# Summing graph messages: one 128-column lane window for each group of edges, in place of one or two block windows

## The chip, the core and the metric

The kernel runs on one core of a Trainium2 chip. The metric is the device time of a whole execution in microseconds; the median of the timed executions counts. A timed execution is not recorded. The profile comes from one further execution, recorded by the hardware profiler, whose own time is given beside its span below.

The engines are named as in the profile: PE (TensorE's matmuls) and PEld (its weight loads), DVE (VectorE), ACT (ScalarE), POOL (GpSimd), SP (SyncE, which here issues most of the DMAs).

## What is computed

A graph has 6250 nodes with 64 features and E = 206250 directed edges, sorted by destination. Four layers run one after another, each on the normalized output of the one before and each with a residual sum. The third is the one that matters here. It has a message for every edge, made of the edge's own 64 attributes and a transformed row of its source node, and takes for each node the root of the mean of the squared messages:

```python
Vp = jax.nn.leaky_relu(V @ pAw + pAb, NEG_SLOPE) @ pBw + pBb
x = jax.nn.relu(E @ mlp_w1 + mlp_b1)
x = jax.nn.relu(x @ mlp_w2 + mlp_b2)
scale = jax.nn.sigmoid(x @ Bw + Bb)
shift = x @ Cw + Cb
msg = scale * Vp[src] + shift
M = jnp.power(jnp.clip(msg, EPS, None), ALPHA)          # ALPHA = 2
ssum = jax.ops.segment_sum(M, dst, num_segments=n)
mean = ssum / jnp.maximum(cnt, 1.0)[:, None]
return jnp.power(mean, 1.0 / ALPHA)
```

The other three layers multiply node features by the graph's adjacency matrix (with degree norms); the last one does so three times.

## The kernel before

**Nodes, blocks and strips.** The 6250 nodes are padded to NP = 49 x 128: NB = 49 blocks of 128 nodes, in NC = 7 chunks of CB = 7 blocks. A node is a block and a lane (0 to 127) in it. The adjacency counts are first built as a dense bf16 matrix in DRAM, in 14 strips of 448 columns (A, made by L926 to L947). Layers one and two, and the last two rounds of layer four, go through the whole matrix with `gather`, whose matmuls are those of L733. A float32 feature block is held as three bf16 parts, so each product takes three matmuls.

**The edge loop.** Layer three runs over G = 202 groups of 128 x 8 = 1024 edges. It is a hand-made software pipeline: `slot(i)` issues, in a fixed order for PE, ACT and DVE (`manual_schedule`), one step of each of several groups. In slot i, SP loads the attributes of group i+2; POOL gathers the source rows of group i in eight indirect DMAs of 128 rows (`fetched`, L1226, into v, which has four buffers); PE transposes group i's attributes (L1234), does the first layer for group i-1 and the second for group i-2 (L1238), then gates and shifts for group i-3 (`gates_and_shifts`, L1248 and L1252, into p_bc, which has one buffer of two banks). DVE and ACT make the message of group i-4: L1261 multiplies gate and v and frees v, L1262 adds the shift and frees p_bc, L1263 clips, L1268 and L1269 square, L1320, L1321 and L1331 split the square into three bf16 parts (m3).

**The sum over nodes.** Edges are sorted by destination, so a group's nodes lie close together. `window(g)` gives the first block that a group can touch and how many (one or two), from the mean number of edges for each node and a margin DRIFT of 32 nodes. Before the loop, `rel_b` is made: the destination of each edge less the first node of its window, so 0 to 255 (L1077 to L1095, with a check that no edge lies outside). `compared_nodes` (L1274) compares it with a ramp of 256 (or 128) columns and gives a 0/1 matrix of 8 x 256 (or 8 x 128). In `summed`, a slot later, PE multiplies these columns by m3, in eight matmuls for each block (L1286), and accumulates in PSUM: each block has a p_s bank of its own (two in rotation), which stays open over all groups that touch the block. After the last of these, L1290 adds the three parts into H. With a chunk's last block, `finished` norms the chunk and makes it ready for layer four.

**Work beside it.** The loop carries other work, listed in `todo` and spread over the slots by `some_of`: checking that the matrix is symmetric (`crossed`: seven or fourteen transposes of L1137 into p_sum, then L1143 on DVE compares them with a piece of A), and the first round of layer four for the chunks that are done (`partial`: 21 matmuls of L733 into p_sum, then L1157 or L1159 adds to Y). p_sum has one bank. The piece and there tiles for it are loaded by SP. Of these there are 196 checks and 84 partial sums. How many are put into a slot depends on `ends`, the slot in which the next chunk is finished.

The slot's order on the three engines, as far as the change touches it, is: L1261 to L1263, transposes, readers of p_sum, first layer, squares, some of `todo`, L1274, L1320, L1321, second layer, gates and shifts, evictions, L1331, readers of p_sum, the rest of `todo`, `summed`.

[...]

Of the kernel before, what the change touches and what calls it, by code (L numbers as in the profile page):

```python
# [8 lines left out]
F32 = mybir.dt.float32  # L9
BF16 = mybir.dt.bfloat16  # L10
# [3 lines left out]
OP = mybir.AluOpType  # L14
AX = mybir.AxisListType

P = 128
N = 6250
D = 64
NB = 49  # L20
NP = NB * P
CB = 7
# [3 lines left out]
J = 8  # L26
G = -(-E // (P * J))
# [564 lines left out]
CW = 448  # L592
CS = NP // CW
SG = 8
DRIFT = 32


def window(g):

    per = N / E  # L600
    lo = max(int(g * P * J * per) - DRIFT, 0) // P
    hi = min(int((g + 1) * P * J * per) + DRIFT, NP - 1) // P
    return lo, hi - lo + 1


@with_exitstack
def fast(ctx, tc, bad, x, src, dst, edge_attr, W3, b3, W4, b4, w1, b1, w2, b2, Bw, Bb, Cw, Cb,
# [432 lines left out]
    with ExitStack() as ph:  # L1040
# [37 lines left out]
        width = tpool.tile([P, G], F32, name="width")  # L1078
        for t, value in ((origin, lambda g: window(g)[0] * P), (width, lambda g: window(g)[1] * P)):
            g0 = 0  # L1080
            for g in range(1, G + 1):
                if g == G or value(g) != value(g0):
                    nc.gpsimd.memset(t[:, g0:g], float(value(g0)))  # L1083
                    g0 = g
        rel = tpool.tile([P, G, J], F32, name="rel")
        nc.vector.tensor_tensor(rel, dst_g, origin.unsqueeze(2).to_broadcast([P, G, J]),
                                op=OP.subtract)
        rel_b = cpool.tile([P, G, J], BF16, name="rel_b")
        nc.vector.tensor_copy(rel_b, rel)
        off = tpool.tile([P, G, J], F32, name="off")  # L1090
        nc.vector.tensor_tensor(off, rel, width.unsqueeze(2).to_broadcast([P, G, J]), op=OP.is_ge)
        nc.vector.tensor_scalar(rel, rel, 0.0, None, op0=OP.is_lt)
        nc.vector.tensor_add(off, off, rel)
        nc.vector.tensor_reduce(missed[:, 1:2], off.rearrange("p g j -> p (g j)"), axis=AX.X,
                                op=OP.add)  # L1095
        count = cpool.tile([P, 2 * P, J], BF16, name="count")
        nc.gpsimd.iota(count, pattern=[[1, 2 * P], [0, J]], base=0, channel_multiplier=0,
                       allow_small_or_imprecise_dtypes=True)

        before.close()  # L1100
        mpool = ph.enter_context(tc.tile_pool(name="mpool", bufs=3))
        ps_a = ph.enter_context(tc.tile_pool(name="ps_a", bufs=1, space=PSUM))
        ps_s = ph.enter_context(tc.tile_pool(name="ps_s", bufs=2, space=PSUM))
        n1 = stat.tile([P, NB], F32, name="n1")
        nc.vector.tensor_scalar_max(n1, deg_dst, 1.0)
        nc.vector.reciprocal(n1, n1)
# [17 lines left out]
        def crossed(n, i, k, b):  # L1124
            if b % ROWS == 0:
                held["there"] = mpool.tile([P, ROWS, 2, CW], BF16, name="there", bufs=2)
                m = min(ROWS, CB - b)
                for h in range(2):
                    nc.sync.dma_start(held["there"][:, :m, h, :],
                                      A[2 * i + h][:, k * CB + b:k * CB + b + m, :])  # L1130

            p = ps_a.tile([P, 512], F32, name="p_sum").bitcast(BF16).rearrange(
                "p (a q) -> p a q", q=P)[:, :CB, :]
            for q in (slice(0, P),) if b != CB // 2 else (slice(0, D), slice(D, P)):
                half, lo = divmod(b * P + q.start, CW)
                for a in range(CB):
                    nc.tensor.transpose(p[q, a, :], held[half][:, a, lo:lo + q.stop - q.start],  # L1137
                                        ident_b)
            there = held["there"][:, b % ROWS].rearrange("p h w -> p (h w)")

            def compared():
                junk = mpool.tile([P, CB * P], BF16, name="junk", bufs=1)
                nc.vector.scalar_tensor_tensor(  # L1143
                    junk, p.rearrange("p a q -> p (a q)"), 0.0, there, op0=OP.add,
                    op1=OP.not_equal, accum_out=unlike[:, n:n + 1])

            return compared

        def partial(i, s):

            p = ps_a.tile([P, 512], F32, name="p_sum")
            for b in range(CB):
                spread(p, U3, i * CB + b, held[s % 2][:, b, :], CW, i * CB, CB)

            def added():
                if i == 0:
                    nc.vector.tensor_copy(Y[:, s, :], p[:, :CW])  # L1157
# [47 lines left out]

        plan(FIRST, False)
        last = {b: g for g in range(G) for b in range(window(g)[0], sum(window(g)))}
        ends = [last[c * CB + CB - 1] for c in range(NC)]
        acc = {}

        BC_AT, M_AT, SUM_AT = 3, 4, 5
        of = [{} for _ in range(G)]
        ends = [e + SUM_AT for e in ends]

        def loaded(g):
            of[g]["e"] = mpool.tile([P, J * D], F32, name="e")
# [49 lines left out]
            nc.scalar.activation(m, m, AF.Square)  # L1269

        def compared_nodes(g):
            nb = window(g)[1]
            to = of[g]["to"] = mpool.tile([P, 2 * P, J], BF16, name="to")
            nc.vector.tensor_tensor(  # L1274
                to[:, :nb * P, :], count[:, :nb * P, :],
                rel_b[:, g, :].unsqueeze(1).to_broadcast([P, nb * P, J]), op=OP.is_equal)

        def summed(g):
            b0, nb = window(g)
            m3, to = of[g].pop("m3"), of[g].pop("to")  # L1280
            for b in range(b0, b0 + nb):
                begins = b not in acc
                if begins:
                    acc[b] = ps_s.tile([P, 512], F32, name="p_s")
                for j in range(J):
                    nc.tensor.matmul(acc[b][:, :3 * D], to[:, (b - b0) * P:(b - b0 + 1) * P, j],  # L1286
                                     m3[:, j].rearrange("p t f -> p (t f)"),
                                     start=(begins and j == 0), stop=(last[b] == g and j == J - 1))
# [48 lines left out]
        loaded(0)  # L1337
        loaded(1)
        with tc.manual_schedule(engines={ET.PE, ET.Activation, ET.DVE}):
            for i in range(G + SUM_AT):  # L1340
                slot(i)
            read_them()

# [101 lines left out]
```

## Time and profile before

| | |
|---|---|
| timed executions | 3750.78, 3750.81, 3745.49 us; median 3750.78 |
| recorded execution | 4268.4 us, span 4266.6 us |
| mean granted TensorE clock, recorded | 0.863 of full speed; 0.80 from 1132 to 3749 us |
| first gather of the edge loop starts | 1132.5 us |
| last gather of the edge loop ends | 3748.9 us |
| last sum over nodes, L1290 | 3779.3 us |
| busy from 1132 to 3749 us (2617 us) | PE 1889.5, DVE 1146.7, ACT 863.9, POOL 1632.4 us |

The recorded execution is 518 us longer than the timed ones, so a sum made from its durations has to be carried over. The profile's group rows read: line, engine, operation, output and inputs with sizes, count, then busy time and mean nanoseconds of one, then the idle time of the engine just before them and what ended most of it. "issue" is a wait that nothing in the profile explains. A row of waits gives the total, the number and the longest; a row of the timeline gives start, length, engine, line, operation, count, and in brackets the idle time before it.

The edge loop is the middle of the page's forty slices, some 12th to 35th: PE's digit is 6 or 7 there, DVE's and POOL's are 4 and 6, and the granted clock moves between 0.6 and 0.8. In the stretches before and after, PE is at 9 with L733.

### The profile page before, as it was taken

To read this page: it belongs to the slowest core of one execution; us is meant where nothing else is said; L and a number is where in the kernel's file an instruction comes from. 1 tells how busy PE (TensorE), PEld (TensorE's weight loads), DVE (VectorE), ACT (ScalarE), POOL (GpSimd) and SP (SyncE) were. 2 spreads that over 40 slices of the span, in tenths; PEclk is the share of its full clock that TensorE was granted. 3 is DMA by queue.
4 is the path that set the end of the run, shared out by engine and by line. 5 is a ranking of instruction groups with operands and counts; after the bars stand their busy time and mean duration, and the time that the engine had idled before them with its cause. 6 is when DMAs were issued, how large, how long until landed. Compare 5 with 4: busy or idle time off the path is not lost.

```text
span 4266.6 us, 59486 instructions
## 1 busy us (share of the span) xinstructions
PE 3314.6 (78%) x24499; PEld 1988.6 (47%) x24499; DVE 1874.4 (44%) x3013; ACT 1305.6 (31%) x2108; POOL 1693.1 (40%) x1822
## 2 busy tenths in 40 slices
PE   0599989999476767677677777677777777789999
PEld 0366656555233434444443444344444444456665
DVE  5999942311243444435444444444444444450100
ACT  0577740111033333333333333333333333320000
POOL 4000000000366666655665666566566656610000
PEclk9799999999677778888887888788878878799999
DMA  3244449778732223333233333233323323269997
GB/s 103 90 187 173 198 202 421 288 319 339 106 82 73 73 69 92 83 100 85 72 98 85 88 85 103 67 86 89 99 71 102 96 76 88 73 231 369 376 363 299
DMA packets 278029, 650.45 MB, mean 152 GB/s; under 512 B 106505, under 2 KB 158787, under 8 KB 275699
## 3 DMA queue, kind: packets, MB, share of 16 engines
q1 hardware_dynamic: 220036, 584.91, 37.9%
q0 software_dynamic: 54112, 58.92, 7.3%
q8 instruction: 194, 3.18, 0.3%
q10 hardware_dynamic: 3600, 2.73, 0.3%
q14 instruction: 87, 0.71, 0.1%
HBM read 562.82 MB, written 83.58 MB: 152 GB/s over the span
## 4 chain that ended last, share of the span: by engine, by line
PE 56%; DVE 13%; issue 13%; another core or an unknown queue 8%; ACT 4%; DMA 3%; POOL 2%; DVEq 0%; ACTq 0%; SPq 0%; POOLq 0%
PE p_sum L733 28%; PE p_bc L1252 7%; PE p L1238 6%; PE p_s L1286 5%; PE p_a L935 3%; PE p_bc L1248 2%; DVE junk L1143 2%; DVE m L1261 2%; PE p_node L724 2%; PE p_e L1234 2%; DVE m L1262 2%; PE p_sum L1137 1%; POOL v L1226 1%; ACT h L1242 1%
## 5 line engine op out<-in xcount | busy, mean ns | idle before, releaser
L1226 POOL DMA_INDIRECT v<-Vp_dram,src_g x1616 | 1632.4, 1010 | 1019.9 <-DVE m L1261 510.6
L733 PE MATMUL p_sum<-piece,U 128*64 128x448 bf16 x10290 | 1111.0, 368 | 194.9 <-issue 133.4
L733 PEld LDWEIGHTS <-U 128*64 128x64 bf16 x12348 | 721.5, 113 | 728.0 <-issue 254.3
L1252 PE MATMUL p_bc<-BC,h 128*128 128x256 f32 x1616 | 534.6, 451 | 57.7 <-issue 56.2
L1286 PE MATMUL p_s<-m,to 128*128 128x192 bf16 x2816 | 352.9, 279 | 119.4 <-issue 118.7
L1252 PEld LDWEIGHTS p_bc<-BC,h 128*128 128x128 f32 x1616 | 308.9, 212 | 206.9 <-issue 179.9
L1083 POOL MEMSET origin<- 128x4 f32 (+3 forms) x49 | 1.7, 100 | 970.6 <-PE p_sum L733 970.6
L1286 PEld LDWEIGHTS <-to 128*128 128x128 bf16 x2816 | 301.1, 150 | 178.3 <-issue 172.1
L1261 DVE TENSOR_TENSOR m<-gate,v 128x512 f32<-128x512 f32 x202 | 139.9, 692 | 503.9 <-ACT gate L1257 288.1
L1242 ACT ACTIVATE h<-p,b_c 128x512 f32<-128x512 f32 x404 | 262.4, 685 | 245.9 <-remote 172.5
L939 ACT ACTIVATE strip<-p_a 128x784 bf16<-128x784 f32 x392 | 301.6, 820 | 89.8 <-PE p_a L935 88.5
L1143 DVE SCALAR_TENSOR_TENSOR junk<-p_sum,there 128x896 bf16<-128x896 bf16 x196 | 212.5, 1084 | 263.2 <-remote 196.1
L1238 PE MATMUL p<-h,w_d 128*128 128x512 f32 x404 | 254.7, 714 | 75.0 <-ACT h L1242 50.5
L1137 PE MATMUL p_sum<-ident_b,piece 128*128 128x128 bf16 (+1 forms) x1568 | 134.8, 235 | 209.8 <-DVE junk L1143 133.9
L1268 ACT ACTIVATE m<-m 128x512 bf16<-128x512 f32 x202 | 127.3, 630 | 505.8 <-DVE m L1263 398.4
L1137 PEld LDWEIGHTS <-piece 128*128 128x128 bf16 (+1 forms) x1568 | 108.5, 109 | 322.3 <-issue 265.9
L1238 PE MATMUL p<-eT,w_d 128*128 128x512 f32 x404 | 241.2, 679 | 16.4 <-issue 12.4
L1321 ACT ACTIVATE m<-m 128x512 bf16<-128x512 f32 x202 | 127.2, 630 | 370.3 <-DVE m L1320 285.7
L974 ACT ACTIVATE y<-p_sum 128x448 f32<-128x448 f32 x56 | 30.5, 544 | 678.7 <-PE p_sum L733 678.7
L926 DVE TENSOR_TENSOR lo<-count,key 128x2048 bf16<-128x2048 bf16 x196 | 238.1, 1215 | 0.0
L733 PE MATMUL p_sum<-strip,U 128*64 128x448 bf16 x2058 | 236.0, 358 | 0.4 <-ACT strip L939 0.4
L1274 DVE TENSOR_TENSOR to<-count,rel_b 128x2048 bf16<-128x2048 bf16 (+1 forms) x202 | 218.2, 1080 | 0.0
(172 smaller groups left out, 2993.8 us busy)
## 6 DMA issues: line engine op xcount, KB each, us to landing
piece<-A SPq DMA_DIRECT2D x498, 784.0 KB
A<-strip SPq DMA_DIRECT2D x14, 5488.0 KB
e<-in_edge_attr SPq DMA_DIRECT2D x202, 256.0 KB
v<-Vp_dram,src_g POOLq DMA_INDIRECT x1616
there<-A SPq DMA_DIRECT2D x56, 448.0 KB
there<-A SPq DMA_DIRECT2D x56, 336.0 KB
pairs<-pair SPq DMA_DIRECT2D x1, 1616.0 KB
Vp_dram<-v SPq DMA_DIRECT2D x7, 224.0 KB
```

The costliest lines, as they stand in the source:

```text
L733: nc.tensor.matmul(p[half * D:(half + 1) * D, :w], U3[:, b, k, :], at_block, start=(i < 2), stop=(i >= 3 * n - 2))
L926: nc.vector.tensor_tensor(t, of.unsqueeze(1).to_broadcast(t.shape), key[:, k, at:at + GB].rearrange("p (h j) -> p h j", j=GQ) .unsqueeze(2 ...
L939: nc.scalar.activation(strip[:, :, col:col + 2 * SG].rearrange("p b (j l) -> p b j l", l=2), p[:, :, :2 * NB].rearrange("p j (b l) -> p b ...
L1137: nc.tensor.transpose(p[q, a, :], held[half][:, a, lo:lo + q.stop - q.start], ident_b)
L1143: nc.vector.scalar_tensor_tensor(junk, p.rearrange("p a q -> p (a q)"), 0.0, there, op0=OP.add, op1=OP.not_equal, accum_out=unlike[:, n:n ...
L1226: nc.gpsimd.indirect_dma_start(out=v[:, j, :], out_offset=None, in_=Vp_dram[:, :], in_offset=bass.IndirectOffsetOnAxis(ap=src_g[:, g, j:j ...
L1238: nc.tensor.matmul(of[g][p], w, of[g].pop(x), start=True, stop=True)
L1242: nc.scalar.activation(of[g][t], of[g].pop(p), **how)
L1252: nc.tensor.matmul(p_bc[:, 2 * q:2 * q + 2].rearrange("p j o f -> p (j o f)"), h2[:, q * P:(q + 1) * P], BC, start=False, stop=(k == 1))
L1261: nc.vector.tensor_mul(m, of[g].pop("gate"), of[g].pop("v"))
L1274: nc.vector.tensor_tensor(to[:, :nb * P, :], count[:, :nb * P, :], rel_b[:, g, :].unsqueeze(1).to_broadcast([P, nb * P, J]), op=OP.is_equal)
L1286: nc.tensor.matmul(acc[b][:, :3 * D], to[:, (b - b0) * P:(b - b0 + 1) * P, j], m3[:, j].rearrange("p t f -> p (t f)"), start=(begins and j ...
```

## The change

A group's window is now always 128 nodes wide and begins at a multiple of QN = 32 nodes. It covers one block, or the end of one and the beginning of the next (`halves`). The 0/1 matrix is made by the lane of the node in its own block (`lane`, 0 to 127, the same for either block), with 128 columns for every group. Eight matmuls sum the group into one PSUM bank, starting and stopping with the group. In the next slot (ADD_AT = 6, one after SUM_AT = 5), DVE adds the three parts into a tile r and adds r, times a mask, to one block of H or to two. The masks (`own`) hold one or zero for each lane: from the window's first lane on, a lane belongs to the first block, below it to the second. The first addition to a block writes it.

p_s becomes one bank, taken from the pool of the others, and p_sum gets two. `finished` is called in the slot after the last sum, behind `summed`. The loop has one slot more, and `ends` moves by one.

```diff
 def window(g):
     per = N / E
-    lo = max(int(g * P * J * per) - DRIFT, 0) // P
-    hi = min(int((g + 1) * P * J * per) + DRIFT, NP - 1) // P
-    return lo, hi - lo + 1
+    lo = max(int(g * P * J * per) - DRIFT, 0) // QN
+    hi = min(int((g + 1) * P * J * per) + DRIFT, NP - 1) // QN
+    assert hi - lo < P // QN
+    return lo
+
+def halves(g):
+    b, q = divmod(window(g), P // QN)
+    return [(b, q, P // QN)] + [(b + 1, 0, q)] * (q > 0 and b + 1 < NB)
...
-        rel_b = cpool.tile([P, G, J], BF16, name="rel_b")
-        nc.vector.tensor_copy(rel_b, rel)
         off = tpool.tile([P, G, J], F32, name="off")
-        nc.vector.tensor_tensor(off, rel, width.unsqueeze(2).to_broadcast([P, G, J]), op=OP.is_ge)
+        nc.vector.tensor_scalar(off, rel, float(P), None, op0=OP.is_ge)
...
+        nc.vector.tensor_scalar(dst_g, dst_g, P - 1, None, op0=OP.bitwise_and)
+        lane = cpool.tile([P, G, J], BF16, name="lane")
+        nc.vector.tensor_copy(lane, dst_g)
+        own = cpool.tile([P, P // QN, 2], F32, name="own")
+        nc.vector.memset(own[:, :, 0], 0.0)
+        for q in range(P // QN):
+            nc.vector.memset(own[q * QN:(q + 1) * QN, :q + 1, 0], 1.0)
+        nc.vector.tensor_scalar(own[:, :, 1], own[:, :, 0], -1.0, 1.0, op0=OP.mult, op1=OP.add)
...
-        ps_s = ph.enter_context(tc.tile_pool(name="ps_s", bufs=2, space=PSUM))
...
-            p = ps_a.tile([P, 512], F32, name="p_sum")
+            p = ps_a.tile([P, 512], F32, name="p_sum", bufs=2)
...
         def compared_nodes(g):
-            nb = window(g)[1]
-            to = of[g]["to"] = mpool.tile([P, 2 * P, J], BF16, name="to")
+            to = of[g]["to"] = mpool.tile([P, P, J], BF16, name="to")
             nc.vector.tensor_tensor(
-                to[:, :nb * P, :], count[:, :nb * P, :],
-                rel_b[:, g, :].unsqueeze(1).to_broadcast([P, nb * P, J]), op=OP.is_equal)
+                to, count, lane[:, g, :].unsqueeze(1).to_broadcast([P, P, J]), op=OP.is_equal)

         def summed(g):
-            b0, nb = window(g)
+            p = of[g]["p_s"] = ps_a.tile([P, 512], F32, name="p_s")[:, :3 * D]
             m3, to = of[g].pop("m3"), of[g].pop("to")
-            for b in range(b0, b0 + nb):
-                begins = b not in acc
-                if begins:
-                    acc[b] = ps_s.tile([P, 512], F32, name="p_s")
-                for j in range(J):
-                    nc.tensor.matmul(acc[b][:, :3 * D], to[:, (b - b0) * P:(b - b0 + 1) * P, j],
-                                     m3[:, j].rearrange("p t f -> p (t f)"),
-                                     start=(begins and j == 0), stop=(last[b] == g and j == J - 1))
-                if last[b] == g:
-                    nc.vector.tensor_reduce(
-                        H[:, b, :], acc[b][:, :3 * D].rearrange("p (t f) -> p f t", f=D),
-                        axis=AX.X, op=OP.add)
-                    if b % CB == CB - 1:
-                        finished(b // CB)
+            for j in range(J):
+                nc.tensor.matmul(p, to[:, :, j], m3[:, j].rearrange("p t f -> p (t f)"),
+                                 start=(j == 0), stop=(j == J - 1))
+
+        begun = set()
+
+        def added_to_nodes(g):
+            r = mpool.tile([P, D], F32, name="r_s")
+            nc.vector.tensor_reduce(r, of[g].pop("p_s").rearrange("p (t f) -> p f t", f=D),
+                                    axis=AX.X, op=OP.add)
+            for k, (b, q0, q1) in enumerate(halves(g)):
+                part = own[:, q1 if k else q0, k:k + 1]
+                if b in begun:
+                    nc.vector.scalar_tensor_tensor(H[:, b, :], r, part, H[:, b, :],
+                                                   op0=OP.mult, op1=OP.add)
+                else:
+                    nc.vector.tensor_scalar(H[:, b, :], r, part, None, op0=OP.mult)
+                    begun.add(b)
+            return [b // CB for b, _, _ in halves(g) if last[b] == g and b % CB == CB - 1]
...
                 nc.vector.tensor_sub(m, m, m3[:, :, 0, :])
                 nc.scalar.activation(m3[:, :, 1, :], m, AF.Copy)
+            done = added_to_nodes(i - ADD_AT) if at(ADD_AT) else []
             if at(2):
                 layer(i - 2, w2_d, "h1", "p_2")
...
             if at(SUM_AT):
                 summed(i - SUM_AT)
+            for c in done:
+                finished(c)
```

More of the change, by code (lines that the diff above doesn't have):

```diff
@@ L594 @@
 SG = 8
+QN = 32
 DRIFT = 32
@@ L1077, in fast @@
         origin = tpool.tile([P, G], F32, name="origin")
[L1078 to L1084, printed above, removed]
+        g0 = 0
+        for g in range(1, G + 1):
+            if g == G or window(g) != window(g0):
+                nc.gpsimd.memset(origin[:, g0:g], float(window(g0) * QN))
+                g0 = g
         rel = tpool.tile([P, G, J], F32, name="rel")
@@ L1095, in fast @@
                                 op=OP.add)
-        count = cpool.tile([P, 2 * P, J], BF16, name="count")
-        nc.gpsimd.iota(count, pattern=[[1, 2 * P], [0, J]], base=0, channel_multiplier=0,
+        nc.vector.tensor_scalar(dst_g, dst_g, P - 1, None, op0=OP.bitwise_and)
[6 more added lines that the diff above has]
+        nc.vector.tensor_scalar(own[:, :, 1], own[:, :, 0], -1.0, 1.0, op0=OP.mult, op1=OP.add)
+        count = cpool.tile([P, P, J], BF16, name="count")
+        nc.gpsimd.iota(count, pattern=[[1, P], [0, J]], base=0, channel_multiplier=0,
                        allow_small_or_imprecise_dtypes=True)
@@ L1130, in crossed @@
                                       A[2 * i + h][:, k * CB + b:k * CB + b + m, :])
-            p = ps_a.tile([P, 512], F32, name="p_sum").bitcast(BF16).rearrange(
+            p = ps_a.tile([P, 512], F32, name="p_sum", bufs=2).bitcast(BF16).rearrange(
                 "p (a q) -> p a q", q=P)[:, :CB, :]
@@ L1206, in fast @@
         plan(FIRST, False)
-        last = {b: g for g in range(G) for b in range(window(g)[0], sum(window(g)))}
+        last = {b: g for g in range(G) for b, _, _ in halves(g)}
         ends = [last[c * CB + CB - 1] for c in range(NC)]
-        acc = {}
-        BC_AT, M_AT, SUM_AT = 3, 4, 5
+        BC_AT, M_AT, SUM_AT, ADD_AT = 3, 4, 5, 6
         of = [{} for _ in range(G)]
-        ends = [e + SUM_AT for e in ends]
+        ends = [e + ADD_AT for e in ends]
         def loaded(g):
@@ L1339, in fast @@
         with tc.manual_schedule(engines={ET.PE, ET.Activation, ET.DVE}):
-            for i in range(G + SUM_AT):
+            for i in range(G + ADD_AT):
                 slot(i)
```

## The prediction

> **What bounds the kernel now.** I read the page first (engines, slices), then the groups of line 5, POOL's waits, the timeline of single slots of the edge loop, and the windows of the loop. The loop is where the change lies: it runs from the first row gather at 1132.5 us to 3790 us, 207 slots, one group of 1024 edges each.
>
> ```profile
> span 4266.6 us, 59486 instructions
> PE 3314.6 (78%) x24499; PEld 1988.6 (47%) x24499; DVE 1874.4 (44%) x3013; ACT 1305.6 (31%) x2108; POOL 1693.1 (40%) x1822
> ...
> L1226 POOL DMA_INDIRECT v<-Vp_dram,src_g x1616 | 1632.4, 1010 | 1019.9 <-DVE m L1261 510.6
> ...
> L1286 PE MATMUL p_s<-m,to 128*128 128x192 bf16 x2816 | 352.9, 279 | 119.4 <-issue 118.7
> ...
> L1137 PE MATMUL p_sum<-ident_b,piece 128*128 128x128 bf16 (+1 forms) x1568 | 134.8, 235 | 209.8 <-DVE junk L1143 133.9
> ...
> L1274 DVE TENSOR_TENSOR to<-count,rel_b 128x2048 bf16<-128x2048 bf16 (+1 forms) x202 | 218.2, 1080 | 0.0
> ```
>
> To see here: the matmuls that the change halves (L1286) are 2816 of 24499, PE also waits on one p_sum buffer (133.9 us behind the comparison L1143), and POOL's 1616 gathers have 1020 us of gaps, half of them waits for a v buffer. The next two views are POOL's waits and POOL's timeline near the end of the loop, where nothing holds it.
>
> ```profile
> POOL v L1226 <- DVE m L1261: 510.6, 95, 18.8
> POOL v L1226 <- issue: 453.0, 1457, 2.4
> ```
>
> ```profile
> 3732.55 0.95 POOL L1226 DMA_INDIRECT v<-Vp_dram,src_g  x1 [0.30 <-issue]
> 3733.81 0.94 POOL L1226 DMA_INDIRECT v<-Vp_dram,src_g  x1 [0.30 <-issue]
> 3735.05 0.95 POOL L1226 DMA_INDIRECT v<-Vp_dram,src_g  x1 [0.30 <-issue]
> 3736.31 1.46 POOL L1226 DMA_INDIRECT v<-Vp_dram,src_g  x1 [0.30 <-issue]
> 3738.07 0.95 POOL L1226 DMA_INDIRECT v<-Vp_dram,src_g  x1 [0.30 <-DVE m L1262]
> 3739.32 1.63 POOL L1226 DMA_INDIRECT v<-Vp_dram,src_g  x1 [0.30 <-issue]
> ```
>
> A gather goes out every 1.25 us, so POOL alone needs 8 x 1.25 = 10.0 us a slot, 2020 us in all, and 123 us more for gathers that last over 0.945 us (like the 1.46 and 1.63 above). In the recorded execution a slot takes 2617 / 202 = 13.0 us, because PE is late: in its timeline there are stretches where matmuls start at steps of some 0.70 us with nothing to wait for, each 10 to 20 us long:
>
> ```profile
> 2185.84 0.24 PE L1286 MATMUL p_s<-m,to 128*128 128x192 bf16 x1 [0.79 <-issue]
> 2186.54 0.39 PE L1286 MATMUL p_s<-m,to 128*128 128x192 bf16 x2 [0.46 <-issue]
> ...
> 2195.87 1.54 PE L1286 MATMUL p_s<-m,to 128*128 128x192 bf16 x16
> ```
>
> The same 16 matmuls take 1.54 us when PE runs freely (a whole slot then lasts 8 us: transposes at 2189.26, the next at 2197.25).
>
> **Recorded and timed execution differ, and this decides the forecast.** The recorded one took 4268.4 us, the timed ones 3750.8: 518 us less. Which execution is bound by what? Take POOL's waits for v buffers out of the recorded span: 4266.6 - 511 = 3756 us. Or build it up: 1132.5 before the first gather, 2020 of gathers at full pace, 517.7 from the last gather's end (3748.9) to the end: 3670, and 80 us of lengthened gathers reach the timed 3750. So I read the timed execution as one in which POOL hardly ever waits (10.4 us a slot) and PE, with some 8 us of work at full clock, has 2 us to spare. This is an inference from two sums, not a record of a timed run.
>
> [...] I laid each gather's start against VectorE's instructions in the timeline. Of 155 gathers that started while L1274 ran, 154 were lengthened, 76.6 us in all, each by about what was left of L1274; L1320, L1261 and L1331 (also two SBUF inputs) add 24 us. Of 163 that started in L1143, whose one input is in PSUM, 2 were. [...] the granted clock changes in multiples of 3.4 us between 0.5 and 1.0, with a mean of 0.80 in the loop.
>
> **The change, part by part**, for 202 groups. From the two forms of window(): 150 groups now have two blocks and 52 one (352 x 8 = 2816 matmuls); after, each has one set of 8, 1616, and 352 halves are added (49 of them first writes).
>
> PE: 1200 matmuls of L1286 with their loads go. 16 take 1.54 us at full clock (0.096 each) and 2.76 at half clock (0.172): 115 to 206 us; by the row, 1200 x 352.9/2816 = 150. A second p_sum bank (taken from p_s[...]) removes most of the 134 + 47 us for which L1137 and L733 wait for L1143. In the recorded execution, where PE is late, I expect 150 plus about half of 181, and the pace is then PE's own: 4266 - 240 = some 4030. In the timed one PE's share is hidden by POOL.
>
> DVE: the comparison L1274 falls from 218.2 to 202 x 0.684 (its 1024-element form) = 138, -80. The reduction of p_s runs 202 times in place of 49: 153 x 0.358 = +55. 303 scalar_tensor_tensor and 49 tensor_scalar on 64 elements are new; the trace has none so small, L688 takes 0.625 for 448 elements [...] from below 0.17 (the 7-element L680), from above 0.36 (as L1290): +79. In sum +54, 0.27 us a slot. They stand between L1320 and L1331, where DVE waits 0.70 us for ACT's L1321 in nearly every slot, so this covers most of it; uncovered it would be 0.8 us on a DVE that is 44% busy.
>
> New waits: the reduction waits for PE's sums of the slot before; behind it on DVE stand L1331 and the readers of p_sum. Those sums take 0.9 us and were issued before the transposes of the new slot, while DVE has three passes, L1143, L1274 and L1320 to do: no wait as a rule, at worst 0.5. PE's next sums wait for the reduction because p_s has one bank; ahead of them stand p_bc's 2.8 us on PE, about as long as DVE needs from L1262 to the reduction (0.43 + 1.3 of ACT + 0.69 + 0.36). I take 0, at worst 0.8 us a slot, with the next slot's transposes queued behind; POOL's 2 us cover that. At the end there is one slot more: +1 us, against 4 tail slots that lose 0.7 each: -2.
>
> Before the loop: rel_b's cast (0.98) goes, the width compare becomes a tensor_scalar (1.83 to 0.99), a bitwise and (1 to 1.8), a cast (0.98) and six tiny instructions come (0.6 to 1): +0 to +1.5 on the wait of the first gather. 194 memsets replace 49 + 97, done during the 8.6 us load of dst_g.
>
> POOL, the bound: where POOL is always running, a DVE instruction of length d, shorter than the pitch, lengthens gathers by d*d/(2 x 1.25) on average. L1274 before: 150 x 0.593 + 52 x 0.187 = 98.7, of which the trace shows 76.6; after: 202 x 0.187 = 37.8, scaled alike 29. Gain 47. The bound from below is 0 (the phase is fixed by when the rows land, and may be one where both lengths cost alike), from above 0.54 x 150 = 81. The new scalar_tensor_tensor have two SBUF inputs: 303 x 0.020 = 6, at most 68. Together -41, with +1 before the loop and -2 at the end: about -43. Timed: 3750.8 - 43 = 3708.
>
> **Rivals.**
> A (forecast), POOL's pace is the bound, 3708, own range 3675 to 3738. For it: both sums above. Against: 1.25 us a gather may be shorter when nothing records. Chance 0.52.
> B, PE sets the pace in timed runs too. Then PE's 150 and part of 181 count: -120 to -220, 3580 as its value. For it: 728 us in which PE is not busy in the loop's 2617, and the clock, in the recorded run. Against: 8 us of work a slot against 10. Chance 0.18.
> C, nothing to see: the lengthening only moves from L1274 to L1320, which now starts in its place, within 0.2%: 3750. Chance 0.11.
> D, slower: [...] PE gets 0.6 us less work a slot and new short waits ahead of its sums, idles longer in each 10.4 us slot[...]. The 8.0 us slot above becomes 8.3 on the mean (84 x 2.27 / 202 = 0.9 more for L733, 0.2 less for L1286, 0.4 less for its 14 transposes), and 7.7 after the change: PE fits under POOL down to a granted clock of 0.74; at 0.70 a slot takes 11.0, 0.6 x 202 = 120 us, less A's 43: 3828. For it: half clock in a fifth to a half of each stretch already. [...] Chance 0.19.
>
> **How the numbers follow.** I can tell 0.2% (7.5 us) from no change. Faster: 0.48 of A, B's 0.18, 0.02 of C: 0.68. Same: 0.04 of A and 0.08 of C: 0.12. Slower: 0.01 of C and D: 0.20. The range for 8 in 10 takes A and C whole, B down to 3585 and D up to 3795.
>
> **What would show it.** Right: L1286 with 1616 matmuls; L1274 all at 0.68; POOL's gathers over 0.96 us fewer, their mean down from 1010 to about 985 ns; L1137's wait on L1143 nearly gone; a recorded span near 4030, with POOL's waits on L1261 down by more than half. Wrong: a mean gather unchanged (C); a timed gain over 100 us (B); a lower granted clock in the loop, L1286 waiting for the new reduction, and POOL still waiting for L1261 (D).

## The result, and the profile after

| | before | after |
|---|---|---|
| median of 4 executions | 3750.14 us (3745.49 to 3750.81) | 3725.39 us (3719.05 to 3728.70) |
| ratio after / before | | 0.9932, 95% interval 0.9918 to 0.9947 |
| forecast | | 3708 us, a ratio of 0.989 |

The change gains 24.75 us, 0.7%. The forecast was a gain of 43 us. The recorded execution of the changed kernel (3727.58 us) is one of its four. The recorded execution shown of before (4268.4 us) was of a kind that one chip later showed in every execution of the three kernels that ran on it, so the profile after is set beside a second record of the kernel before, e0_before_again, whose execution took 3742.60 us (span 3740.8).

The page of the changed kernel: span, engines with busy time and instructions, then rows of groups (busy, mean ns of one, idle time before and what ended most of it).

```profile
span 3725.9 us, 57673 instructions
...
PE 3092.7 (83%) x23299; PEld 1853.5 (50%) x23299; DVE 1890.3 (51%) x3525; ACT 1282.9 (34%) x2108; POOL 1666.7 (45%) x1870
...
L1238 POOL DMA_INDIRECT v<-Vp_dram,src_g x1616 | 1606.2, 994 | 529.1 <-issue 460.8
...
L1260 PE MATMUL p_bc<-BC_b,ones 3*128 3x512 bf16 x404 | 182.0, 450 | 359.4 <-DVE m L1274 358.8
...
L1292 PE MATMUL p_s<-m,to 128*128 128x192 bf16 x1616 | 202.7, 278 | 1.1 <-DVE r_s L1300 0.4
```

The same rows of the page of e0_before_again:

```profile
span 3740.8 us, 59486 instructions
...
PE 3142.0 (84%) x24499; PEld 1914.6 (51%) x24499; DVE 1856.7 (50%) x3013; ACT 1290.4 (34%) x2108; POOL 1684.1 (45%) x1822
...
L1226 POOL DMA_INDIRECT v<-Vp_dram,src_g x1616 | 1623.4, 1005 | 528.0 <-issue 450.7
...
L1286 PE MATMUL p_s<-m,to 128*128 128x192 bf16 x2816 | 286.3, 256 | 0.0
...
L1248 PE MATMUL p_bc<-BC_b,ones 3*128 3x512 bf16 x404 | 177.3, 439 | 117.3 <-DVE m L1262 117.2
L1137 PE MATMUL p_sum<-ident_b,piece 128*128 128x128 bf16 (+1 forms) x1568 | 128.8, 235 | 174.3 <-DVE junk L1143 174.2
...
L1274 DVE TENSOR_TENSOR to<-count,rel_b 128x2048 bf16<-128x2048 bf16 (+1 forms) x202 | 219.2, 1085 | 0.0
```

PE lost 1200 matmuls and its 174 us wait for the single p_sum bank behind the comparison of L1143 (after, none is left at the transposes and 0.3 us at L742), and has in their place 242 us more of waiting for p_bc (117.2 to 358.8): what PE was relieved of, it waits for DVE at another place. The row that the span follows is POOL's. Its gathers fell from 1005 to 994 ns on the mean, in sum by 1623.4 - 1606.2 = 17.2 us. POOL's waits after the change (total, number of times, longest) show that nothing holds it:

```profile
POOL v L1238 <- issue: 460.8, 1512, 0.3
...
POOL v L1238 <- DMA piece<-A: 37.0, 1, 37.0
POOL v L1238 <- DMA v<-Vp_dram,src_g: 25.6, 84, 0.3
```

The 37.0 us stand once, ahead of the first gather. No other wait is longer than the 0.3 us before every gather, so none was for a buffer of v. So the span can be cut at the first start and the last end of the gathers, and the loop between them into the time by which gathers last over 0.945 us ("lengthening") and the rest. This works for every record taken where the kernel before takes 3750 us; the experiments are explained below.

| record, us | first gather | lengthening | rest of the loop | after the last gather | span |
|---|---|---|---|---|---|
| e0_before_again | 1126.2 | 98.4 | 2017.2 | 499.1 | 3740.8 |
| after | 1128.0 | 81.0 | 2017.4 | 499.5 | 3725.9 |
| e1_wide_compare | 1127.8 | 99.5 | 2017.1 | 497.3 | 3741.7 |
| e2_dve_time_one_input | 1127.7 | 66.6 | 2017.2 | 497.4 | 3708.9 |
| e3_matmuls_back | 1125.4 | 84.2 | 2017.3 | 503.5 | 3730.4 |
| e4_one_p_sum | 1125.8 | 75.3 | 2017.2 | 500.7 | 3719.0 |
| e6_compare_one_input | 1126.2 | 66.6 | 2017.2 | 501.4 | 3711.4 |
| e8_m_in_psum | 1126.7 | 30.9 | 2016.8 | 497.6 | 3672.1 |
| e9_both | 1125.1 | 15.2 | 2016.8 | 498.5 | 3655.7 |
| e11_both_again | 1128.1 | 17.5 | 2016.8 | 498.5 | 3660.9 |
| e12_gate_again | 1125.2 | 8.3 | 2016.7 | 499.6 | 3649.8 |

The rest of the loop is the same 2017 us in all of them, 1.248 us for each of 1616 gathers, whatever was done to PE and DVE. Between e0 and after the lengthening makes -17.3, the first gather +1.8 and the end +0.4, together with rounding the -15.0 us of the two spans. The medians differ by 10 us more: the recorded execution of e0 lay 7.5 us under the 3750.14, that of after 2.2 us over its own median.

To see which instruction lengthens a gather, each gather is put down to the DVE instruction that runs when it starts (where one is still ending when the next has begun, to the later one; the 76.6 us of the prediction are counted in the same way):

| lengthening, us, by the pass that runs | e0 | after | e1 | e2 | e6 | e8 | e9 | e12 |
|---|---|---|---|---|---|---|---|---|
| comparison (L1274, now L1285) | 64.2 | 23.2 | 70.2 | 24.1 | 12.1 | 18.7 | 1.8 | 2.4 |
| first remainder (L1320, now L1336) | 12.2 | 25.7 | 7.4 | 16.4 | 21.4 | 0 | 0 | 0 |
| second remainder (L1331, now L1348) | 5.3 | 12.6 | 3.2 | 8.9 | 14.3 | 0 | 0 | 0 |
| gate times message (L1261, now L1273) | 11.1 | 13.2 | 13.6 | 11.0 | 12.7 | 8.9 | 8.7 | 0 |
| all others | 5.6 | 6.4 | 5.1 | 6.3 | 6.1 | 3.2 | 4.7 | 5.9 |

The comparison gives up 41.0 us, and 20.8 of it come back in the two remainders (the two subtractions that leave what the first and the second bf16 part don't hold). The timelines show how. This is one slot of e0 (start, length, engine, line; POOL's and DVE's lines alone):

```profile
1832.43 1.21 DVE L1274 TENSOR_TENSOR to<-count,rel_b 128x2048 bf16<-128x2048 bf16 x1
...
1832.56 1.89 POOL L1226 DMA_INDIRECT v<-Vp_dram,src_g  x1 [0.30 <-issue]
...
1833.87 0.69 DVE L1320 TENSOR_TENSOR m<-m,m 128x512 f32<-128x512 f32 x1 [0.23 <-ACT m L1269]
...
1834.76 0.94 POOL L1226 DMA_INDIRECT v<-Vp_dram,src_g  x1 [0.30 <-issue]
```

The gather that starts 0.13 us into the long comparison is held for 0.95 us. It ends at 1834.45, and the next one starts 0.2 us after L1320 has ended (1834.56): no gather starts in L1320, which costs nothing here. And one slot of the kernel after:

```profile
2222.85 0.69 DVE L1285 TENSOR_TENSOR to<-count,lane 128x1024 bf16<-128x1024 bf16 x1
...
2223.36 0.99 POOL L1238 DMA_INDIRECT v<-Vp_dram,src_g  x1 [0.30 <-issue]
2224.29 0.69 DVE L1336 TENSOR_TENSOR m<-m,m 128x512 f32<-128x512 f32 x1 [0.76 <-ACT m L1281]
2224.66 1.15 POOL L1238 DMA_INDIRECT v<-Vp_dram,src_g  x1 [0.30 <-issue]
...
2225.68 0.69 DVE L1348 TENSOR_TENSOR m<-m,m 128x512 bf16<-128x512 f32 x1
2226.11 1.08 POOL L1238 DMA_INDIRECT v<-Vp_dram,src_g  x1 [0.30 <-issue]
```

Here the comparison costs 0.04 us, but the next gather starts inside L1336 (+0.21), and the one after inside L1348 (+0.14). The second of these follows from the first. A gather that L1336 holds is followed by another start 1.12 us after the end of L1336, while L1348 begins 0.70 us after that end. So the next gather starts 0.42 us into L1348 and is held for 0.138 us, every time that L1336 has caught a gather: 38 times in e0 (5.25 us), 91 times after (12.56 us). In both passes the gather lasts longer by what was left of the pass less 0.13 us.

The rows of DVE after, shapes kept apart, give the durations of the new and shortened work:

```profile
L1348 DVE TENSOR_TENSOR m<-m,m 128x512 bf16<-128x512 f32 x202 | 139.3, 690 | 6.8 <-ACT m L1337 1.4
...
L1285 DVE TENSOR_TENSOR to<-count,lane 128x1024 bf16<-128x1024 bf16 x202 | 139.0, 688 | 0.0
...
L1305 DVE SCALAR_TENSOR_TENSOR H<-r_s,own,H 128x64 f32<-128x64 f32 x303 | 77.4, 283 | 7.1
L1300 DVE TENSOR_REDUCE r_s<-p_s 128x64 f32<-128x192 f32 x202 | 70.8, 351 | 0.2 <-PE p_s L1292 0.2
```

L1348, which as L1331 had 140.6 us of waits for ACT in e0, has 6.8 us of idle time before it left: the reduction and the additions lie in that wait.

### The profile page after: what moved, and what is told of

Same layout as the page of the kernel before. It is cut to its first block, busy times and chain, and to the rows that moved or that the text cites. A ratio compares the mean times of both kernels' runs of the same rounds, so it can differ in the third digit from the quotient of the medians.

```text
span 3725.9 us, 57673 instructions
## 1 busy us (share of the span) xinstructions
PE 3092.7 (83%) x23299; PEld 1853.5 (50%) x23299; DVE 1890.3 (51%) x3525; ACT 1282.9 (34%) x2108; POOL 1666.7 (45%) x1870
## 4 chain that ended last, share of the span: by engine, by line
PE 35%; POOL 32%; issue 14%; DMA 9%; DVE 8%; ACT 2%; POOLq 0%; DVEq 0%; ACTq 0%; SPq 0%
POOL v L1238 32%; PE p_sum L742 26%; DMA v<-Vp_dram,src_g 6%; PE p_a L944 3%; PE p_node L733 2%; DVE hd L935 1%; DVE lo L935 1%; PE p_bc L1264 1%; DMA dst_g<-in_dst 1%; DMA piece<-A 1%; DVE m L1273 0%; DVE m L1274 0%; PE p_node L915 0%; DVE junk L849 0%; PE p_node L725 0%
## 5 line engine op out<-in xcount | busy, mean ns | idle before, releaser
L1238 POOL DMA_INDIRECT v<-Vp_dram,src_g x1616 | 1606.2, 994 | 529.1 <-issue 460.8
L742 PE MATMUL p_sum<-piece,U 128*64 128x448 bf16 x10290 | 1051.7, 360 | 20.0 <-issue 9.9
L742 PEld LDWEIGHTS <-U 128*64 128x64 bf16 x12348 | 694.9, 111 | 527.5 <-issue 95.5
L1264 PE MATMUL p_bc<-BC,h 128*128 128x256 f32 x1616 | 603.6, 509 | 0.0
L1273 DVE TENSOR_TENSOR m<-gate,v 128x512 f32<-128x512 f32 x202 | 140.0, 693 | 798.1 <-DMA v<-Vp_dram,src_g 567.5
L1260 PE MATMUL p_bc<-BC_b,ones 3*128 3x512 bf16 x404 | 182.0, 450 | 359.4 <-DVE m L1274 358.8
L1280 ACT ACTIVATE m<-m 128x512 bf16<-128x512 f32 x202 | 127.3, 630 | 990.7 <-DVE m L1275 990.7
L1264 PEld LDWEIGHTS p_bc<-BC,h 128*128 128x128 f32 x1616 | 349.7, 240 | 157.6 <-issue 117.1
L1260 PEld LDWEIGHTS <-ones 3*128 3x128 bf16 x404 | 37.5, 93 | 613.6 <-DVE m L1274 486.2
L1250 PE MATMUL p<-h,w_d 128*128 128x512 f32 x404 | 222.6, 633 | 50.7 <-ACT h L1254 50.7
L742 PE MATMUL p_sum<-strip,U 128*64 128x448 bf16 x2058 | 236.2, 358 | 0.4 <-ACT strip L948 0.4
L1156 DVE SCALAR_TENSOR_TENSOR junk<-p_sum,there 128x896 bf16<-128x896 bf16 x196 | 212.3, 1083 | 12.1 <-PE p_e L1246 9.9
L944 PE MATMUL p_a<-hd,lo 128*128 128x98 bf16 x3136 | 189.5, 214 | 33.3 <-DVE lo L935 31.9
L944 PEld LDWEIGHTS <-lo 128*128 128x128 bf16 x3136 | 160.0, 101 | 103.4 <-DVE lo L935 81.5
L1292 PE MATMUL p_s<-m,to 128*128 128x192 bf16 x1616 | 202.7, 278 | 1.1 <-DVE r_s L1300 0.4
```

Source lines behind the costliest of these rows:

```text
L742: nc.tensor.matmul(p[half * D:(half + 1) * D, :w], U3[:, b, k, :], at_block, start=(i < 2), stop=(i >= 3 * n - 2))
L944: nc.tensor.matmul(p[:, j, :2 * NB], lo[:, g // GQ, :, g % GQ], hd[:, g // GQ, :, g % GQ], start=True, stop=True)
L1156: nc.vector.scalar_tensor_tensor(junk, p.rearrange("p a q -> p (a q)"), 0.0, there, op0=OP.add, op1=OP.not_equal, accum_out=unlike[:, n:n ...
L1238: nc.gpsimd.indirect_dma_start(out=v[:, j, :], out_offset=None, in_=Vp_dram[:, :], in_offset=bass.IndirectOffsetOnAxis(ap=src_g[:, g, j:j ...
L1250: nc.tensor.matmul(of[g][p], w, of[g].pop(x), start=True, stop=True)
L1260: nc.tensor.matmul(p_bc[:, 4 * b:4 * b + 4].rearrange("p j o f -> p (j o f)"), ones, BC_b, start=True, stop=False)
```

## The experiments

The theory: in the timed executions POOL sets the pace, and the time changes only by how long DVE passes with two inputs in SBUF hold up gathers (98.4 us in the record of e0, 81.0 after, by the column of lengthening). The rivals: DVE's busy time itself, PE's matmuls, p_sum's banks. All kernels are edits of the changed one except the first; "..." stands for lines left out. Ratios are against the kernel before on the same chip. The expectations call this theory A. The records show which gathers are held and for how long, and not why.

**The kernel before, recorded once more.**

> The kernel before, unchanged, for a second record of it. Theory A (POOL's pace bounds the loop): the record comes out near 3750 us, the gathers follow one another every 1.25 us or a little more without waiting for a v buffer, and their mean is 1000 to 1010 ns; the first record, 4268 us, was a disturbed one. Theory B (PE sets the pace): again well over 3750 us, or near 3750 with POOL waiting for L1261 for hundreds of us.

Measured: 3742.6 us. Once the loop runs, gathers never wait for a buffer; a slot takes 10.47 us. What the prediction had inferred of the timed executions from two sums is now in a record.

**The comparison as wide as before.** In 151 groups 256 columns are compared, of which PE uses 128.

```diff
+            wide = P if g % 4 == 0 else 2 * P
...
-                to, count, lane[:, g, :].unsqueeze(1).to_broadcast([P, P, J]), op=OP.is_equal)
+                to[:, :wide, :], count[:, :wide, :],
+                lane[:, g, :].unsqueeze(1).to_broadcast([P, wide, J]), op=OP.is_equal)
```

> The changed kernel, but the comparison makes 256 columns in 151 of the 202 groups (128 of them unused) and 128 in the others, as in the kernel before; all else as changed. Theory A[...]: the gathers get longer again by about 0.4 us in each of the 151 slots scaled by 0.78, 40 to 60 us in sum, so 3725 + 20 to 60. Theory C (the lengthening only moves to the next instruction): 3725 within 8 us.

Measured: 3751.78 us, ratio 1.0009 (1.0001 to 1.0017). The page's row of POOL:

```profile
L1238 POOL DMA_INDIRECT v<-Vp_dram,src_g x1616 | 1624.4, 1005 | 527.4 <-issue 453.8
```

The width of this one pass accounts for the whole gain of the change: with it back, the gathers' mean is the 1005 ns of before, though PE's 1200 matmuls are still gone and p_sum has two banks. In the table the comparison is up by 47 us and the remainders are down by 27.7: the trade between them runs both ways. In sum the gathers of the record last 18.5 us longer, and not the 40 to 60 that were expected: the expectation had left this trade out.

**The same time on DVE without a second input.** In the same 151 groups a reduction of 384 elements, whose result nobody uses, follows the comparison.

```diff
...
+            if g % 4:
+                nc.vector.tensor_reduce(
+                    spent[:, g:g + 1], count[:, :48, :].rearrange("p a j -> p (a j)"),
+                    axis=AX.X, op=OP.max)
```

> The changed kernel with one more DVE instruction after the comparison in 151 groups, a reduction of 384 elements with a single SBUF input, about 0.56 us, as long as what the wide comparison adds. Theory A: it does not hold up POOL, and DVE has time to spare: 3725 within 8 us. If it is DVE's time [...] that counts: as much longer as the wide comparison.

Measured: 3709.1 us, ratio 0.9891 (0.9877 to 0.9906). The row of the added instruction:

```profile
L1289 DVE TENSOR_REDUCE spent<-count 128x1 f32<-128x384 bf16 x151 | 82.1, 544 | 0.0
```

It is the length that e1 had added to the comparison (1219 - 686 = 533 ns), in the same place, and it costs nothing. The time is even 16 us below the changed kernel's, where at most 8 had been expected (66.6 us of lengthening in place of 81.0). The first remainder (L1336) starts 1.07 us after the comparison's start in place of 0.91 (medians) and catches 64 gathers in place of 91. A place in the slot is worth that much, so a pass cannot be priced by its length alone.

**The matmuls given back.** In 151 groups the eight matmuls are issued twice; the second set starts the sum again.

```diff
-            for j in range(J):
+            for _ in range(2 if g % 4 else 1):
+                for j in range(J):
...
```

> The changed kernel with the eight matmuls of a group's sum issued twice in 151 groups (the second set overwrites the first), so that PE has its 1200 matmuls back. Theory A: hidden in the loop, 2 to 4 us for the slots after the last gather: 3725 to 3732. Theory B: 115 to 206 us longer.

Measured: 3729.2 us, ratio 0.9942 (0.9930 to 0.9955). The page's row of these matmuls:

```profile
L1293 PE MATMUL p_s<-m,to 128*128 128x192 bf16 x2824 | 297.5, 262 | 6.8 <-DVE r_s L1301 6.4
```

1208 matmuls, 95 us by the rows, move the time by at most a few us; the interval overlaps that of the result. PE is busy 1728.5 us of the 2090 from 1130 to 3220 us, against 1676.5 after and 1719.0 in e0: it has room in all three.

**One bank for p_sum.** The line that differs is the buffer count, once for the checks and once for the partial sums.

```diff
-            p = ps_a.tile([P, 512], F32, name="p_sum", bufs=2)
+            p = ps_a.tile([P, 512], F32, name="p_sum")
```

> The changed kernel with one p_sum bank in place of two. Theory A (POOL's gathers bound the loop and PE has time to spare): 3725 within 8 us. Theory B (PE's waits on p_sum are part of the gain): up to 180 us longer, at least 20.

Measured: 3721.01 us, ratio 0.9925 (0.9912 to 0.9939). PE's waits:

```profile
PE p_sum L1150 <- DVE junk L1156: 197.9, 83, 6.5
PE p_bc L1260 <- DVE m L1274: 139.1, 64, 5.6
```

The wait that the second bank had removed is back in full, and the wait for p_bc is 220 us shorter. What PE doesn't wait for DVE at one place it waits at the other: 337 us in 147 waits here, 358.8 us in 132 after. The bank is worth nothing here and can be used for something else.

**The comparison with one input in SBUF.** One lane column at a time is compared as a scalar: eight instructions of 128 columns in place of one. The lanes are float32 for this, and the matrix is laid out so that PE reads 128 adjacent elements.

```diff
-            nc.vector.tensor_tensor(
-                to, count, lane[:, g, :].unsqueeze(1).to_broadcast([P, P, J]), op=OP.is_equal)
+            for j in range(J):
+                nc.vector.tensor_scalar(to[:, j, :], count, lane[:, g, j:j + 1], None,
+                                        op0=OP.is_equal)
...
```

> The changed kernel with the comparison made by eight tensor_scalar of 128 columns (one SBUF input each and a scalar for each partition) in place of one tensor_tensor with two SBUF inputs; the same result. Theory A [...]: the 20.7 us by which the comparison lengthens gathers go, and the comparison takes DVE about 0.6 us more in each slot, which shifts L1336 and L1348; between 20 us shorter and 15 us longer than 3725, with no gather lengthened by the comparison itself. [...] eight of them lengthen gathers by as much or more, 3725 to 3745.

The range from 3725 to 3745 is for the case that eight tensor_scalar instructions hold gathers too. Measured: 3713.46 us, ratio 0.9903 (0.9888 to 0.9918), lengthening 66.6 us. The comparison's column says 12.1 us, but 11.3 of this are 19 gathers that started in the last of the eight instructions, 0.03 to 0.06 us before L1336 (here L1337) began, and lasted 1.53 to 1.57 us, as long as if L1337 had held them. It takes both instructions: in the next kernel but one (e9), where L1337's counterpart has one input in PSUM, 13 gathers start at this place and none is longer by over 0.03 us; and of 521 gathers that start within 0.075 us ahead of another two-input pass, in seven records, none is held. What happens between the two is open. The other gathers that start in the comparison cost 0.8 us in all. The other passes keep the rest, so alone this edit gains little.

**The remainders with one input in SBUF.** The clipped message is written to the bank that p_sum gave back, so that L1336 and L1348 read one input from PSUM.

```diff
-            p = ps_a.tile([P, 512], F32, name="p_sum", bufs=2)
+            p = ps_a.tile([P, 512], F32, name="p_sum")
...
-            nc.vector.tensor_scalar_max(m, m, EPS)
+            of[g]["m"] = ps_a.tile([P, J, D], F32, name="p_m")
+            nc.vector.tensor_scalar_max(of[g]["m"], m, EPS)
```

> The changed kernel with one p_sum bank, and the clipped message m in a PSUM bank of its own, so that L1336 and L1348 have one SBUF input each. Theory A [...]: the 38 us that these two add to gathers go, some of it coming back on the comparison: 15 to 40 us under the changed kernel, 3685 to 3710. If the place in time and not the input counts: 3725 within 8 us.

Measured: 3675.01 us, ratio 0.9803 (0.9790 to 0.9816). The rows of the two passes on DVE:

```profile
L1337 DVE TENSOR_TENSOR p_m<-p_m,m 128x512 f32<-128x512 f32 x202 | 140.7, 696 | 46.0 <-ACT p_m L1282 41.3
...
L1349 DVE TENSOR_TENSOR m<-p_m,m 128x512 bf16<-128x512 f32 x202 | 138.7, 686 | 5.6 <-ACT m L1338 1.3
```

They are as long as before (0.69 us), and 90 and 93 gathers start in them, against 80 and 80 in e4, of which every one was lengthened. Here none is. Against e4, which has the same single p_sum bank and ran on the same chip, the edit gains 3721.01 - 3675.01 = 46 us; the time lies 10 us below the range that was expected: instead of taking back some of the 31.1 us that the remainders had cost in e4, the comparison's lengthening fell too (29.8 to 18.7). The two passes kept their durations; one operand moved to another memory, and the clipping ahead of them became longer (0.445 to 0.695 us). L1349 still writes to SBUF, so it is the second input there, and not the output, that holds a gather.

**Both.**

> The two edits before together: comparison by tensor_scalar, m in PSUM, one p_sum bank. Of DVE's instructions in a slot only L1273 keeps two SBUF inputs. Theory A [...]: gathers are lengthened by 10 to 25 us in sum in place of 82, so 3655 to 3675. A rival, that DVE with over 7 us of work in a slot becomes late: 3725 or more, with POOL waiting for L1273.

Measured: 3660.47 us, ratio 0.9763 (0.9750 to 0.9776). From the page:

```profile
span 3655.7 us, 59702 instructions
...
PE 3032.8 (83%) x23299; PEld 1814.8 (50%) x23299; DVE 2076.4 (57%) x4939; ACT 1246.6 (34%) x2108; POOL 1598.6 (44%) x1870
...
L1238 POOL DMA_INDIRECT v<-Vp_dram,src_g x1616 | 1539.9, 953 | 530.7 <-issue 444.3
```

DVE is busy 186 us longer than in the changed kernel (2076.4 against 1890.3), and the span is 70 us shorter. DVE's time is not what the loop pays for.

**The gate in PSUM too**, so that the multiplication of gate and message (L1273) has one input in SBUF. ACT writes the gate over the values that it was made from:

```diff
-            gate = of[g]["gate"] = mpool.tile([P, J, D], F32, name="gate")
-            nc.scalar.activation(gate, of[g]["p_bc"][:, :, 0, :], AF.Sigmoid)
+            gate = of[g]["gate"] = of[g]["p_bc"][:, :, 0, :]
+            nc.scalar.activation(gate, gate, AF.Sigmoid)
```

It and the changed kernel ran on a chip on which the kernel before takes 4265.79 us (16 executions, 4246.57 to 4292.15), like the first record of before.

> The version with both edits (3660), and the gate written back to its place in p_bc, so that L1273 too has one SBUF input: none of DVE's large instructions in a slot has two. Theory A [...]: the last 9 us of lengthening in the loop go, 3648 to 3655; a slot of POOL's then takes 10.0 us and nothing is left to gain from DVE. If ACT's write to PSUM is slow or holds p_bc longer: 3660 or more, with POOL still at its pace unless DVE is over 10 us late.

> The changed kernel as it is, beside the others on the same chip, to see how far its runs spread: 3719 to 3730.

Measured there: the gate in PSUM 4284.32 us, ratio 1.0033 (1.0010 to 1.0056); the changed kernel 4243.30 us, ratio 0.9943 (0.9922 to 0.9965). The page of a0_after_again:

```profile
span 4267.2 us, 57673 instructions
...
L1238 POOL DMA_INDIRECT v<-Vp_dram,src_g x1616 | 1613.2, 998 | 1042.3 <-DVE m L1273 533.8
L742 PE MATMUL p_sum<-piece,U 128*64 128x448 bf16 x10290 | 1135.2, 363 | 182.6 <-issue 170.0
...
L1292 PE MATMUL p_s<-m,to 128*128 128x192 bf16 x1616 | 231.2, 283 | 152.4 <-issue 125.0
```

Here POOL waits 534 us for v buffers, and PE has gaps that no wait explains. Fewer matmuls are worth little here too: with 1200 fewer, and two p_sum banks, the time is 22 us shorter, not 240. The kernel with the gate in PSUM shows what lengthening is worth where POOL is not the bound: gathers hardly held up at all (4 us in its record), and no gain. Its single p_sum bank may be what makes it slower (PE waits 319 us for L1156 at L1150); this was not tried apart. Both expectations named a time of the other chips and missed.

The same two kernels, e9's and e10's, on a chip where the kernel before takes 3751.67 us (it was the one that e9_both had run on, so the gain of this pair is shown on one chip alone):

> The kernel of e9_both once more, to see whether its gain holds on a second chip and what it is where the kernel before takes 4266 us. Theory (the pace of the timed loop is POOL's, 1.25 us for a gather that nothing lengthens): where the kernel before takes about 3750 us, 3655 to 3675 us, a ratio of 0.975 to 0.978, with gathers of about 0.95 us and some 12 us of lengthening in all. Where the kernel before takes about 4266 us, POOL is not the pace and the lengthening that it takes away is worth little: 4230 to 4290 us. Rival (the gain of e9 came from fewer vector instructions per block, not from POOL): a gain of about 2% on either kind of chip.

> The kernel of e10_gate_in_psum once more (the gate is written into PSUM, so that the multiplication of gate and message has one input in SBUF). Theory: where the kernel before takes about 3750 us, the 8.8 us of lengthening that e9 had left at that multiplication go, 3645 to 3660 us, 5 to 12 us below e11_both_again in the same call. Rival (holding p_bc longer makes PE late, which then decides): at or above e11_both_again. Where the kernel before takes about 4266 us: again 4270 to 4300.

Measured: 3662.89 us, ratio 0.9770 (0.9754 to 0.9786), and 3650.91 us, ratio 0.9733 (0.9719 to 0.9747). The page of e12_gate_again:

```profile
span 3649.8 us, 59301 instructions
...
L1238 POOL DMA_INDIRECT v<-Vp_dram,src_g x1616 | 1532.9, 949 | 530.8 <-issue 440.7
```

With no pass of two SBUF inputs left among the large ones, the mean gather is 949 ns, 4 over the 945 of a gather that nothing lengthens. This version is faster than both kernels where POOL sets the pace: 101 us less than before, four times the gain of the change.

## Why the prediction was right, and by how much not

The forecast was A, and its mechanism is shown: the loop runs at POOL's pace, and the gain is shorter gathers. The size was 43 us against 24.75 in the medians and 15.0 in the two records. By its own steps:

- **The sum that reached 3750 held by luck in its parts.** It took 1132.5 and 517.7 us ahead of and behind the gathers from the record of 4268 us, 25 us more than e0 has (1126.2 and 499.1), and 80 us of lengthening, which was only what the sum still lacked, 18 less than e0 has (98.4). Nor were the lengthened gathers of the first record 123 us over 0.945; their durations give 106.6. (The parts of the forecast, -41, +1 and -2, make -42.) The bound that it inferred is the right one all the same.
- **The mis-sized term is POOL's sum.** "Gain 47" for L1274 was measured as 41.0 (64.2 to 23.2; the record of 4268 us had shown 76.6, in slots of 13.0 us in place of 10.47). What was taken as zero was the shift to the passes behind: +13.5 in L1336, +7.3 in L1348, +2.1 in L1273. The prediction had named this as rival C, all or nothing, and given it 0.11; half of it happened. The estimate d*d/(2 x 1.25) treats each pass as if it met gathers at random. For L1336, whose last 0.13 us hold nothing, d is 0.56 us, and it gives 202 x 0.314 / 2.5 = 25 us, the 25.7 after; before, the long comparison had shielded it down to 12.2.
- **The additions' own lengthening** was put at 6 us and is 0.07 (2 of 88 gathers that started in L1305). Their duration was the author's estimate, 79 us for 352 of them or 0.224 us each, between the 0.17 and 0.36 us of L680 and L1290 in the record of before; it is 0.283 us. With the 49 first writes this is 12 us more on DVE by the rows (91.3 in place of 79) and, as e2 and e9 show, costs nothing.
- **DVE**: the comparison -80 forecast, -80.2 by the rows; the reduction +55, measured +53.3; covered by the wait for ACT, as said.
- **New waits**: taken as 0, measured 0.2 us (reduction) and 0.4 us (PE's next sums) in all.
- **Before the loop and at the end**: +1 and -2 forecast, +1.8 and +0.4 in the records.
- **PE and p_sum hidden in timed executions**: shown by e3 and e4. PE's time by the rows of L1286 fell by 84 us, less than the 115 to 206 forecast, and in the stretch from 1130 to 3220 us its busy time by 42.5, with the granted clock at 0.85 in place of 0.88.
- **Wrong: "a recorded span near 4030"** in an execution like the first record, with POOL's waits for L1261 down by more than half. The changed kernel takes 4243 us there, and in its record (4269 us, the longest of six) POOL waits 533.8 us where it waited 510.6. The step that failed is that PE's 240 us would come off the span. The waits behind L1143 did go, 181 us to 0.4, and so did 122 us of matmuls (352.9 to 231.2). But from 1132 to 3749 us PE is busy for 1879.2 us, against 1889.5, and so idle for 738, against 728: the other matmuls take 111 us more, at a mean granted clock of 0.76 in place of 0.80, and other waits came. This is the lower clock of rival D, in a record where POOL does wait. What makes all of it longer on that chip stays open.

Rival B falls with e3. Rival D's sign was there, a lower clock (0.85 in place of 0.88 from 1130 to 3220 us), and it decided nothing because PE had the room: 1676.5 us busy of 2090. That the clock would fall with PE's idle time was the author's assumption; no run tested what lowers it.

## What to carry to other kernels

When an engine that runs without a pause sets the pace, look first for what makes its own instructions longer: here the time for which two-input passes held gathers was paid for in full, while 186 us of added DVE work (e9) and 1208 matmuls (e3) cost next to nothing. Don't add such collisions up one by one: shortening one pass uncovers the next, so remove the cause from all of them (an operand in PSUM: 31.1 us of lengthening in e4, none in e8; a scalar in place of a tensor: 18.7 us in e8, 1.8 in e9) or count the collisions in order along the timeline. A buffer that removes a wait on an engine with room is a bank to spend elsewhere.

## What the runs showed of the hardware that was not expected

- Moving one operand of the 0.69 us pass L1336 to PSUM took its lengthening from 20.0 us (e4) to nothing (e8). An operand in PSUM is not always enough: in the record after, the addition of the shift (there L1274), which reads p_bc from PSUM, lengthened 23 of the 108 gathers that started in it, by 1.3 us in sum. The clipping (L1275, a tensor_scalar on 512 float32 elements in SBUF) took 0.445 us on the mean, and 0.695 us in e8 with its output in PSUM; of the 69 gathers that started in it in the record after none was lengthened. What makes it longer there, no trace says.
- The two-input passes L1320 and L1336 held gathers that started while they ran (129 in e0 and after), for what was left of the pass less 0.13 us. Of 521 that started just ahead of such a pass none was held, but for the 19 of e6 behind a tensor_scalar. The other way round nothing was held: L1336 took 0.68 to 0.69 us in all 202 slots, whether a gather runs or not.
- A difference of 14% between chips for one and the same kernel, the one before (3748 and 4266 us), with PE's unexplained gaps and a granted clock of 0.86 to 0.87 in place of 0.91 to 0.92, was larger than any edit's effect.
